# An FFT-convolution block and a four-way scan on one core: big transfers cut into parts on SyncE's queue, a new pace for background work, another order on ScalarE, and softplus operands two slices ahead

## The chip, the cores and the metric

The kernel runs on one core of a Trainium2 chip. The core has five engines with a queue of instructions each: TensorE (PE in the profile, its weight loads PEld), VectorE (DVE), ScalarE (ACT), GpSimd (POOL) and SyncE (SP), which here only issues transfers. 16 DMA engines move data between HBM and the on-chip memory SBUF. PSUM is a second, smaller on-chip memory that TensorE writes. The metric is the device time of one execution in microseconds (us).

## The reference

The input x has shape (16, 64, 64, 96): 16 images, 64 x 64 pixels, 96 channels, float32. Two layers follow, each added to its input.

```
# group norm with 32 groups: gn(x) = (x - mean) / sqrt(var + 1e-5)
# layer 0
xu  = upsample_2x(gn(x))              # by FFT, low-pass
h   = xu @ W1.T + b1                  # 96 -> 384
h   = c0 + c1 * h + c2 * h * h
h   = h @ W2.T + b2                   # 384 -> 96
x   = x + lowpass(h)[::2, ::2]        # by FFT
# layer 1
xz  = gn(x) @ in_proj.T               # 96 -> 2 * 192
u   = silu(conv3x3_depthwise(xz[:192])); z = silu(xz[192:])
# four directions k: rows, columns, and both reversed; L = 4096 steps
dt, B, C = split(x_proj[k] @ u_k)     # 6 + 16 + 16 rows
delta    = softplus(dt_proj[k] @ dt + bias)
h_t = exp(delta_t * A) * h_{t-1} + delta_t * u_t * B_t     # 192 channels x 16 states
y_t = sum over states of h_t * C_t,  + u_t * D
y   = layernorm(sum of the four directions) * z
x   = x + y @ out_proj.T
```

The softplus is computed as max(s, 0) + log(1 + e) with e = exp(-|s|), less the rounding error of 1 + e, which is ((1 + e) - 1) - e.

## The kernel before

**Three kinds of work.** `front(mi)` computes layer 0 of image mi, and of layer 1 the group norm, the projection and the 3x3 convolution; it leaves `xs`, `z` and `x1` in HBM. `scan()` runs the recurrences of all images. `finish(mi)` adds the directions, normalises, multiplies by z and projects out. `front(0)` runs alone before the scan and `finish(15)` alone after it; all the other fronts and finishes run as background inside the scan.

**The scan.** A step is an image, a pair of directions and a piece of 1024 of the 4096 positions: 16 x 2 x 4 = 128 steps. A step has 6 blocks of 64 channels (two directions of 192), a block 4 units of 4 of the 16 states, so there are 3072 units. The loop body of a unit n has two columns, e = 1 (odd) and e = 0, each a tile of 128 (32 channels x 4 states) x 1024 positions. `decay` (L719, ScalarE) makes da = exp(delta * A) in PSUM. `drive` (L725, GpSimd) makes b = dtu * B for both columns, two units ahead. `recur` (L734, L736, VectorE) runs the recurrence over a column: the odd column's result goes into b in SBUF, the even one's into da in PSUM. `keep` (L742, ScalarE) copies the last state, one element a partition, for the next step. The product with C is made by GpSimd in place for the odd column (L863), and by VectorE for the even one (L873). L863 overwrites what `keep` reads, so it waits for it. `read_out` (L758, TensorE) sums over states.

**The order of the work is written out by hand** (a manual schedule): the order of the lines is the order of each engine's queue. The background work is cut into slices, Python generators that yield between slices. `slot()` stands three times in the body of a unit: after the odd column's recurrence, after the even one's, and at the body's end. At each, `Background.slot` runs one slice where the work is behind its pace: `SLICES` slices in `POS` = 576 slots an image for `front` of the next image and then `finish` of the last; and `PSLICES` slices in 58 slots for `project`, the projections of the next step. `drain` runs what is left.

**`project`** (L633 to L671) works on pieces of 512 positions, two a step, and in each on three blocks of 128 rows: 128 x 2 x 3 = 768 blocks. A block is a matmul into `s` (PSUM), Abs and Exp on ScalarE into `e`, Ln into `d`, then on VectorE L657 (d = max(s, 0) + d), on ScalarE L659 (s = e + 1), on VectorE L661 (s = (s - 1) - e), L662 (s = d - s) and L666 (dtu = s * u), and the copy L668. `e` and `d` are in SBUF. The two results go to HBM on SP's queue, and come back spread over partitions through `fetch`.

**Queues of the transfers.** Nearly all transfers are issued by SP. Seven an image, the large ones, are issued by ScalarE: `xt` (L241, 1.5 MB, in runs of 64 elements), the two `s` (L408), `x1` (L431), `col` (L492, 2 MB) and the two `ycol` (L507, L508).

**Norms.** L227 and L252 in `norm` and `front` are small VectorE additions and products of two SBUF tiles, run three times an image.

Of the kernel before, what the change touches and what calls it, by code (L numbers as in the profile page):

```python
# [45 lines left out]
F32 = mybir.dt.float32  # L46
AF = mybir.ActivationFunctionType
ALU = mybir.AluOpType
# [3 lines left out]
C = 96  # L52
HW = 64
# [17 lines left out]
POS = 3 * 8 * 6 * NQ  # L71
SLICES = 404
PSLICES = 60


@with_exitstack
def tile_two_blocks(
    ctx: ExitStack, tc: tile.TileContext,
    x, w1, w1t, b1, w2t, b2, coef, inpt, convw, convb, xpt, dtw, alog, dsk, onw, onb, opt,
    up, down, fold, ident, gmask, pmat, bumps, out,  # L80
# [109 lines left out]
    def piece(shape, name):  # L190
        return b2p.tile(shape, F32, name=name, tag="piece")

    def norm(xt):

        s = small.tile([C, 8], F32, name="gs")
        for t in range(8):
            junk = piece([C, TB], "junk")
            nc.scalar.activation(junk, xt[:, TB * t:TB * t + TB], AF.Identity, accum_out=s[:, t:t + 1])
            if t % 2:
                yield  # L200
        yield
        m_ps = bank([C, 8], "m_ps")
        nc.tensor.matmul(m_ps, lhsT=gmask_s, rhs=s, start=True, stop=True)
        yield
        junk8 = small.tile([C, 8], F32, name="junk8")
        nmean = small.tile([C, 1], F32, name="nmean")
        nc.scalar.activation(junk8, m_ps, AF.Identity, scale=-1.0, accum_out=nmean)
        s2 = small.tile([C, 8], F32, name="gs2")
        for t in range(8):
            junk = piece([C, TB], "junk")  # L210
            nc.scalar.activation(
                junk, xt[:, TB * t:TB * t + TB], AF.Square, bias=nmean, accum_out=s2[:, t:t + 1]
            )
# [12 lines left out]
        yield  # L226
        nc.vector.tensor_mul(nb, nmean, rg)  # L227
        yield
        return rg, nb

    def front(mi):

        x_c = x[mi].rearrange("h c w -> c h w")
        x_h = x[mi]
# [5 lines left out]
        xt = b16.tile([C, L], F32, name="xt", tag="b16")  # L240
        nc.scalar.dma_start(out=xt.rearrange("c (h w) -> c h w", w=HW), in_=x_c)  # L241
        for _ in range(4):
            yield
        rg, nb = yield from norm(xt)
# [200 lines left out]
        for i, n, tiles, both in ((0, 128, 8, 0), (1, 64, 4, 4)):  # L445
            col = b16.tile([128, tiles * TB], F32, name="col", tag="b16")
            parts = [(n * k, t0) for k, t0 in enumerate((0, both)[:128 // n])]
            turned = None

            def turn(t, row, z):  # L450
                nc.scalar.copy(
                    col.rearrange("c (w h) -> c w h", w=HW)[:, :, 8 * t:8 * t + 8],
                    row.rearrange("c (h w) -> c w h", w=HW),
                )
                for p, t0 in parts:
                    cols = slice(TB * (t + t0), TB * (t + t0) + TB)
                    nc.sync.dma_start(out=made["xs"][2 * i, 0:n, cols], in_=row[p:p + n])
                    nc.sync.dma_start(out=made["z"][128 * i:128 * i + n, cols], in_=z[p:p + n])

            for t in range(tiles):  # L460
                c_ps = bank([128, 8, HW], "c_ps")
                for tap in range(9):
                    dy, dx = divmod(tap, 3)
                    for p, t0 in parts:
                        h0 = 8 * (t + t0) + dy
# [10 lines left out]
                for p, t0 in parts:  # L476
                    h0 = 8 * (t + t0) + 1
# [9 lines left out]
                turned = t, row, z  # L487
                yield
            turn(*turned)
            yield  # L490
            if i == 0:
                nc.scalar.dma_start(out=made["xs"][1], in_=col)  # L492
            else:
                for p, t0 in parts:
                    to = made["xs"][2, 64:128, :].rearrange("c (w h) -> c w h", h=HW)
                    for w0 in range(0, HW, 16):
# [3 lines left out]
                        )  # L500
                        yield

    def finish(mi):

        y_d, xs_d, z_d, x1_d = (image[mi][k] for k in ("y", "xs", "z", "x1"))
        ycol = [b18.tile([128, L], F32, name="ycol0", tag="b18"), b16.tile([64, L], F32, name="ycol1", tag="b16")]
        nc.scalar.dma_start(out=ycol[0], in_=y_d[1, 0:128, :])  # L507
        nc.scalar.dma_start(out=ycol[1], in_=y_d[1, 128:DI, :])  # L508

# [9 lines left out]
        ahead = fetch_y(0)  # L519
        for _ in range(6):  # L520
            yield
        tail = None
        for t in range(8):
# [7 lines left out]
            for ob, n in ((0, 128), (1, 64)):  # L531
# [11 lines left out]
                yield  # L543
                for i in range(2):
# [10 lines left out]
                yc.append(y_ps.rearrange("c h w -> c (h w)"))  # L555
                yield

# [3 lines left out]
            nc.tensor.matmul(v_ps, lhsT=mean_s, rhs=sq[0], start=True, stop=False)  # L561
            yield
# [5 lines left out]
            yield  # L568
            r = sq[0][0:C]
# [3 lines left out]
            for i, n in ((0, 128), (1, 64)):  # L573
                nc.tensor.matmul(o_ps, lhsT=ow_s[0:n, i, :], rhs=yz[i], start=(i == 0), stop=(i == 1))
            yield
# [4 lines left out]
            yield  # L580

# [9 lines left out]
        for _ in tail:  # L591
            yield

# [5 lines left out]
    def scan():  # L599


        with ExitStack() as es:
# [12 lines left out]
            def project(mi, pair, lc, out):  # L615
# [7 lines left out]
                for t in range(0, T, TB):  # L623
# [15 lines left out]
                    for i, v in enumerate((0, 2, 1)):  # L639
# [18 lines left out]
                        yield  # L658
                        nc.scalar.activation(s, e, AF.Identity, bias=one_s)  # L659
                        yield  # L660
                        nc.vector.scalar_tensor_tensor(s, s, -1.0, e, ALU.add, ALU.subtract)  # L661
                        nc.vector.tensor_sub(s, d, s)  # L662
                        yield
                        dtu = pj.tile([128, TB], F32, name="dtu")
# [121 lines left out]
            class Background:  # L786


                def __init__(self, gen, slices, positions):
                    self.gen, self.slices, self.positions, self.at, self.n = gen, slices, positions, 0, 0  # L790

                def slot(self):
                    self.at += 1
                    if self.gen is not None and self.n * self.positions < self.at * self.slices:
                        self.n += 1
                        if next(self.gen, 0) == 0:
                            self.gen = None

                def drain(self):
                    while self.gen is not None:  # L800
                        self.n += 1
                        if next(self.gen, 0) == 0:
                            self.gen = None

# [14 lines left out]
            for n, (st, bi, j) in enumerate(units):  # L819
# [43 lines left out]
                nc.gpsimd.tensor_mul(h, h, bc[1, r, j])  # L863
# [82 lines left out]
def _layout(i):  # L946
# [4 lines left out]
    for k in range(ND):  # L951
# [12 lines left out]
    laid = {  # L964
        "x": x,
        "w1": w1.reshape(HB, 128, C).swapaxes(0, 1),
        "w1t": w1.T,
# [35 lines left out]
```

## Time and profile before

| | us |
|---|---|
| median of 3 runs | 22337.41 (22315.87 to 22346.83) |
| the profiled execution | 22310.87 |
| its span, first to last instruction | 22309.1 |
| GpSimd busy | 20896.4 (94%) |
| VectorE busy | 19837.0 (89%) |
| TensorE busy | 15814.4 (71%) |
| ScalarE busy | 13129.1 (59%) |
| before GpSimd's first scan instruction | 532.9 |
| after its last one | 165.6 |
| DMA engines, mean rate | 191 GB/s |

The span is that of one execution, and the executions agree within some 0.15%. A line of a group gives the source line, the engine, the operation, what it writes and reads (with partitions x elements), the count, and then the busy time in us, the mean of one in ns, the idle time of the engine just ahead of these instructions, and what ended that idle time. A line of the timeline gives the start, the duration, the engine and the instruction, and in brackets the idle time before it.

### The profile page before, as it was taken

The page shows a single profiled execution, that of the slowest core. Times are in us where ns is not written, and L with a number is a line of the kernel's source. Part 1 is how long each engine was busy: PE and PEld are TensorE (multiplying, and loading weights), DVE is VectorE, ACT ScalarE, POOL GpSimd, SP SyncE. Part 2 cuts the span into 40 slices and gives each one's busy share as a digit, 9 for nine tenths or more (in the row PEclk, how much of TensorE's full clock was granted, in tenths as well). Part 3 has the DMA queues.
Part 4 walks back from the last instruction along what each step waited for, and adds up shares of the span by engine and source line. Part 5 has one row for each costly group of instructions (what it writes and reads, how often), then busy time and mean ns, then how long its engine had stood idle before and what let it go on. Part 6 is the DMA issues. An engine that isn't in the chain of part 4 may idle for free.

```text
span 22309.1 us, 261027 instructions
## 1 busy us (share of the span) xinstructions
PE 15814.4 (71%) x92844; PEld 6455.6 (29%) x92844; DVE 19837.0 (89%) x12829; ACT 13129.1 (59%) x20854; POOL 20896.4 (94%) x6152
## 2 busy tenths in 40 slices
PE   6675777767778677776777777677786777767745
PEld 4322323223232322323223232332323223232211
DVE  0999999899998999989899898999989999898996
ACT  3665655656556565565656556565565655656543
POOL 0999999999999999999999999999999999999997
PEclk7676777877778677686777878677786776867856
DMA  2555565655656556565655656556565665656654
GB/s 77 185 194 184 191 210 182 209 191 193 206 189 210 184 198 204 190 210 186 203 194 191 210 184 209 192 189 209 189 212 184 201 201 190 210 186 203 211 177 133
DMA packets 1915769, 4276.30 MB, mean 192 GB/s; under 512 B 543454, under 2 KB 642686, under 8 KB 1906206
## 3 DMA queue, kind: packets, MB, share of 16 engines
q1 hardware_dynamic: 1804702, 4086.06, 54.6%
q10 hardware_dynamic: 109760, 173.55, 3.0%
q8 instruction: 731, 11.98, 0.2%
q14 instruction: 576, 4.72, 0.1%
HBM read 3380.58 MB, written 878.18 MB: 191 GB/s over the span
## 4 chain that ended last, share of the span: by engine, by line
POOL 31%; issue 20%; DVE 20%; PE 15%; DMA 8%; ACT 5%; SPq 1%; POOLq 0%; ACTq 0%; DVEq 0%
POOL b L863 15%; POOL b L725 15%; DVE da L736 4%; DVE b L734 4%; DVE da L734 4%; DVE b L736 3%; DVE b L873 3%; PE y L758 2%; PE c_ps L466 2%; DMA u<-xs_d 2%; PE pp L633 2%; ACT da L719 2%; PE yc L535 1%; DMA ct<-rows 1%; PE oe_ps L578 1%
## 5 line engine op out<-in xcount | busy, mean ns | idle before, releaser
L725 POOL TENSOR_TENSOR b<-dtu,bt 128x2048 f32<-128x2048 f32 x3072 | 14000.3, 4557 | 578.3 <-DMA dtu<-dtu_d 531.9
L758 PE MATMUL y<-b,fold_s 128*32 128x256 f32 x49152 | 4865.1, 506 | 4962.9 <-DVE b L873 3489.3
L719 ACT ACTIVATE da<-delta,a_s 128x1024 f32<-128x1024 f32 x6144 | 6855.9, 1116 | 2487.3 <-DVE b L873 1350.0
L863 POOL TENSOR_TENSOR b<-b,ct 128x1024 f32<-128x1024 f32 x3072 | 7323.1, 2384 | 668.3 <-ACT new L742 591.3
L758 PEld LDWEIGHTS y<-b,fold_s 128*32 128x32 f32 x49152 | 1324.5, 127 | 8709.7 <-DVE b L873 4353.2
L873 DVE TENSOR_TENSOR b<-da,ct 128x1024 f32<-128x1024 f32 x3072 | 3750.4, 1221 | 75.1
L736 DVE TENSOR_TENSOR_SCAN b<-da,new,b 128x1024 f32<-128x1024 f32 x1152 | 2697.2, 2341 | 376.5 <-ACT new L742 223.5
L734 DVE TENSOR_TENSOR_SCAN b<-da,new,b 128x1024 f32<-128x1024 f32 x1152 | 2700.9, 2344 | 288.4 <-POOL b L725 283.4
L736 DVE TENSOR_TENSOR_SCAN da<-da,new,b 128x1024 f32<-128x1024 f32 x1152 | 2692.7, 2337 | 108.4 <-ACT da L719 108.4
L734 DVE TENSOR_TENSOR_SCAN da<-da,new,b 128x1024 f32<-128x1024 f32 x1152 | 2693.5, 2338 | 85.3 <-ACT da L719 85.3
L742 ACT COPY new<-da 128x1 f32<-128x1 f32 x2304 | 362.6, 157 | 3347.7 <-DVE b L873 3344.4
L466 PE MATMUL c_ps<-xgp,wtap_s 96*128 96x512 f32 (+1 forms) x4608 | 1676.9, 625 | 119.1 <-ACT row L484 114.5
L643 PE MATMUL s<-pr,dtw_s 128*128 128x512 f32 x1536 | 1202.3, 875 | 244.6 <-ACT delta L668 212.5
L358 PE MATMUL h_ps<-xu,w1t_s 96*128 96x500 f32 x1920 | 1316.4, 798 | 74.3 <-ACT hsq L341 32.8
L633 PE MATMUL pp<-u,xpt_s 128*128 128x512 f32 x1536 | 1061.8, 844 | 372.9 <-DMA u<-xs_d 359.8
L370 PE MATMUL o_ps<-w2c_s,hsq 128*100 128x96 f32 x9600 | 1222.0, 296 | 25.8 <-ACT new L742 15.1
L370 PEld LDWEIGHTS o_ps<-w2c_s,hsq 128*100 128x100 f32 x9600 | 1154.6, 208 | 284.9 <-issue 186.6
L742 ACT COPY new<-b 128x1 f32<-128x1 f32 x2304 | 429.9, 187 | 1058.2 <-DVE b L734 587.7
L657 DVE SCALAR_TENSOR_TENSOR d<-s,d 128x512 f32<-128x512 f32 x768 | 521.8, 679 | 555.6 <-ACT d L655 553.1
L736 DVE TENSOR_TENSOR_SCAN da<-da,b 128x1024 f32<-128x1024 f32 x384 | 876.5, 2282 | 133.5 <-ACT da L719 133.5
L734 DVE TENSOR_TENSOR_SCAN b<-da,b 128x1024 f32<-128x1024 f32 x384 | 876.2, 2282 | 99.3 <-POOL b L725 65.7
L736 DVE TENSOR_TENSOR_SCAN b<-da,b 128x1024 f32<-128x1024 f32 x384 | 876.5, 2283 | 69.8 <-POOL b L725 65.5
(120 smaller groups left out, 18395.2 us busy)
## 6 DMA issues: line engine op xcount, KB each, us to landing
dtu<-dtu_d SPq DMA_DIRECT2D x1536, 512.0 KB
delta<-delta_d SPq DMA_DIRECT2D x1536, 512.0 KB
bt<-rows SPq DMA_DIRECT2D x1024, 512.0 KB
ct<-rows SPq DMA_DIRECT2D x1024, 512.0 KB
u<-xs_d SPq DMA_DIRECT2D x896, 256.0 KB
dtu_d<-dtu SPq DMA_DIRECT2D x768, 256.0 KB
delta_d<-delta SPq DMA_DIRECT2D x768, 256.0 KB
xr<-in_x SPq DMA_DIRECT2D x768, 128.0 KB
```

The lines of the kernel that those rows point to most:

```text
L358: nc.tensor.matmul(h_ps[j], lhsT=w1t_s[:, 128 * j:128 * (j + 1)], rhs=xu.rearrange("c p q -> c (p q)"), start=True, stop=True,)
L370: nc.tensor.matmul(o_ps[:, p, :], lhsT=hsq[j][:, UPS * p:UPS * (p + 1)], rhs=w2c_s[:, j, :], start=(j == 0), stop=(j == HB - 1),)
L466: nc.tensor.matmul(c_ps[p:p + n], lhsT=wtap_s[:, tap, 128 * i:128 * i + n], rhs=xgp[:, h0:h0 + 8, dx:dx + HW], start=(tap == 0), stop=(tap ...
L633: nc.tensor.matmul(pp, lhsT=xpt_s[:, pair, v, :], rhs=u[v], start=(v == 0), stop=(v == 2))
L643: nc.tensor.matmul(s, lhsT=dtw_s[:, pair, v, :], rhs=pr, start=True, stop=True)
L719: nc.scalar.activation(da, ops["delta", n // NQ][:, e, :], AF.Exp, scale=a_s[:, k, g, units[n][2]:units[n][2] + 1])
L725: nc.gpsimd.tensor_mul(b, ops["dtu", n // NQ], bt.unsqueeze(1).to_broadcast([128, 2, T]))
L734: nc.vector.tensor_tensor_scan(out, da, b, before, ALU.mult, ALU.add)
L736: nc.vector.tensor_tensor_scan(out[:, ::-1], da[:, ::-1], b[:, ::-1], before, ALU.mult, ALU.add)
L758: nc.tensor.matmul(y[32 * q:32 * q + 32, e, :], lhsT=fold_s, rhs=b[:, e, QT * q:QT * q + QT], start=(pair == 0 and j == 0 and e == 0), sto ...
L863: nc.gpsimd.tensor_mul(h, h, bc[1, r, j])
L873: nc.vector.tensor_mul(bs[n][:, 0, :], h, bc[1, r, j])
```

## The change

The change has five parts.

1. A new helper `parts` cuts a large transfer into pieces along its columns, issues each on SP's queue and yields after each. `xt`, `x1`, `col` and `ycol` go through it; `s` is cut by a loop of its own, in six. The host lays out x a second time, channels first (`xc`), so that `xt` reads whole rows.
2. Slices of the convolution in `front` and of `finish` yield `HEAVY` = 2 in place of nothing, and `Background` counts what a slice yields, 1 where it yields nothing. `SLICES` goes from 404 to 540.
3. In the unit's body, `keep` of the odd column and the next unit's odd `decay` move ahead of `read_out` and of the first `slot()`.
4. In `project`, ScalarE makes 1 + e right behind Ln, in a new SBUF tile `w` in place of `s`; two empty slices follow; then VectorE makes d and w in one slice, and s = d - w and dtu in the next. A block has 7 slices instead of 8, and `PSLICES` goes from 60 to 53.
5. A local name `parts` in the convolution is renamed `halves`.

```diff
-SLICES = 404
-PSLICES = 60
+SLICES = 540
+HEAVY = 2
+PSLICES = 53
...
+    def parts(out, in_, n=4):
+
+        step = L // n
+        for i in range(n):
+            nc.sync.dma_start(out=out[:, step * i:step * i + step], in_=in_[:, step * i:step * i + step])
+            yield
...
-        nc.scalar.dma_start(out=xt.rearrange("c (h w) -> c h w", w=HW), in_=x_c)
-        for _ in range(4):
-            yield
+        yield from parts(xt, xc[mi])
+        yield
...
-        for i, on in enumerate((slice(0, JS), slice(JS, HW))):
-            nc.scalar.dma_start(out=s[i], in_=s_d[:, on, :])
-        for _ in range(8):
+        for i, n, first in [(0, JS // 4, k * JS // 4) for k in range(4)] + [(1, 10, 0), (1, 10, 10)]:
+            nc.sync.dma_start(out=s[i][:, first:first + n, :], in_=s_d[:, JS * i + first:JS * i + first + n, :])
             yield
+        yield
...
-        nc.scalar.dma_start(out=made["x1"], in_=x1)
+        yield from parts(made["x1"], x1)
...
-                        yield
+                        yield HEAVY
...
-                nc.scalar.dma_start(out=made["xs"][1], in_=col)
+                yield from parts(made["xs"][1], col)
...
-        nc.scalar.dma_start(out=ycol[0], in_=y_d[1, 0:128, :])
-        nc.scalar.dma_start(out=ycol[1], in_=y_d[1, 128:DI, :])
+        yield from parts(ycol[0], y_d[1, 0:128, :])
+        yield from parts(ycol[1], y_d[1, 128:DI, :], 2)
...
-        for _ in range(6):
-            yield
+        for _ in range(2):
+            yield HEAVY
...
-                        e = pj.tile([128, TB], F32, name="e")
-                        d = pj.tile([128, TB], F32, name="d")
+                        e, d, w = (pj.tile([128, TB], F32, name=k) for k in ("e", "d", "w"))
                         nc.scalar.activation(e, s, AF.Abs)
                         nc.scalar.activation(e, e, AF.Exp, scale=-1.0)
                         yield
                         nc.scalar.activation(d, e, AF.Ln, bias=one_s)
+                        nc.scalar.activation(w, e, AF.Identity, bias=one_s)
+                        for _ in range(2):
+                            yield
+                        nc.vector.scalar_tensor_tensor(d, s, 0.0, d, ALU.max, ALU.add)
+                        nc.vector.scalar_tensor_tensor(w, w, -1.0, e, ALU.add, ALU.subtract)
                         yield
-                        nc.vector.scalar_tensor_tensor(d, s, 0.0, d, ALU.max, ALU.add)
-                        yield
-                        nc.scalar.activation(s, e, AF.Identity, bias=one_s)
-                        yield
-                        nc.vector.scalar_tensor_tensor(s, s, -1.0, e, ALU.add, ALU.subtract)
-                        nc.vector.tensor_sub(s, d, s)
-                        yield
+                        nc.vector.tensor_sub(s, d, w)
...
                 def slot(self):
                     self.at += 1
                     if self.gen is not None and self.n * self.positions < self.at * self.slices:
-                        self.n += 1
-                        if next(self.gen, 0) == 0:
-                            self.gen = None
+                        self.step()
+
+                def step(self):
+                    weight = next(self.gen, 0)
+                    if weight == 0:
+                        self.gen = None
+                    else:
+                        self.n += weight or 1
...
                 recur(n, 1, h)
+                keep(n, 1, h)
+                if n < last:
+                    decay(n + 1, 1)
                 if n:
                     read_out(n - 1)
                 slot()
-                keep(n, 1, h)
-                if n < last:
-                    decay(n + 1, 1)
```

More of the change, by code (lines that the diff above doesn't have):

```diff
@@ L78, in tile_two_blocks @@
     ctx: ExitStack, tc: tile.TileContext,
-    x, w1, w1t, b1, w2t, b2, coef, inpt, convw, convb, xpt, dtw, alog, dsk, onw, onb, opt,
+    x, xc, w1, w1t, b1, w2t, b2, coef, inpt, convw, convb, xpt, dtw, alog, dsk, onw, onb, opt,
     up, down, fold, ident, gmask, pmat, bumps, out,
@@ L231, in front @@
     def front(mi):
-        x_c = x[mi].rearrange("h c w -> c h w")
         x_h = x[mi]
@@ L446, in front @@
             col = b16.tile([128, tiles * TB], F32, name="col", tag="b16")
-            parts = [(n * k, t0) for k, t0 in enumerate((0, both)[:128 // n])]
+            halves = [(n * k, t0) for k, t0 in enumerate((0, both)[:128 // n])]
             turned = None
@@ L454, in turn @@
                 )
-                for p, t0 in parts:
+                for p, t0 in halves:
                     cols = slice(TB * (t + t0), TB * (t + t0) + TB)
@@ L463, in front @@
                     dy, dx = divmod(tap, 3)
-                    for p, t0 in parts:
+                    for p, t0 in halves:
                         h0 = 8 * (t + t0) + dy
@@ L473, in front @@
                     if tap % 3 == 2 and tap < 8:
-                        yield
+                        yield HEAVY
                 z_ps = bank([128, 8, HW], "z_ps")
-                for p, t0 in parts:
+                for p, t0 in halves:
                     h0 = 8 * (t + t0) + 1
@@ L487, in front @@
                 turned = t, row, z
-                yield
+                yield HEAVY
             turn(*turned)
-            yield
+            yield HEAVY
             if i == 0:
-                nc.scalar.dma_start(out=made["xs"][1], in_=col)
+                yield from parts(made["xs"][1], col)
             else:
-                for p, t0 in parts:
+                for p, t0 in halves:
                     to = made["xs"][2, 64:128, :].rearrange("c (w h) -> c w h", h=HW)
@@ L500, in front @@
                         )
-                        yield
+                        yield HEAVY
     def finish(mi):
@@ L519, in finish @@
         ahead = fetch_y(0)
-        for _ in range(6):
-            yield
+        for _ in range(2):
+            yield HEAVY
         tail = None
@@ L542, in finish @@
                     nc.scalar.activation(sq[0], yc[0], AF.Square)
-                yield
+                yield HEAVY
                 for i in range(2):
@@ L555, in finish @@
                 yc.append(y_ps.rearrange("c h w -> c (h w)"))
-                yield
+                yield HEAVY
             v_ps = bank([C, TB], "v_ps")
@@ L561, in finish @@
             nc.tensor.matmul(v_ps, lhsT=mean_s, rhs=sq[0], start=True, stop=False)
-            yield
+            yield HEAVY
             yz.append(piece([64, TB], "yz"))
@@ L567, in finish @@
                 ahead = fetch_y(t + 1)
-            yield
+            yield HEAVY
             r = sq[0][0:C]
@@ L574, in finish @@
                 nc.tensor.matmul(o_ps, lhsT=ow_s[0:n, i, :], rhs=yz[i], start=(i == 0), stop=(i == 1))
-            yield
+            yield HEAVY
             e_ps = bank([C, TB], "oe_ps")
@@ L579, in finish @@
             nc.vector.tensor_mul(r, o_ps, r)
-            yield
+            yield HEAVY
             def end(r, e_ps, cols):
@@ L591, in finish @@
         for _ in tail:
-            yield
+            yield HEAVY
     blocks = [(0, 0, 0), (0, 2, 0), (2, 0, 0), (2, 2, 1), (1, 0, 1), (1, 2, 1)]
@@ L655, in project @@
                         nc.scalar.activation(d, e, AF.Ln, bias=one_s)
-                        yield
-                        nc.vector.scalar_tensor_tensor(d, s, 0.0, d, ALU.max, ALU.add)
-                        yield
-                        nc.scalar.activation(s, e, AF.Identity, bias=one_s)
-                        yield
-                        nc.vector.scalar_tensor_tensor(s, s, -1.0, e, ALU.add, ALU.subtract)
-                        nc.vector.tensor_sub(s, d, s)
-                        yield
+                        nc.scalar.activation(w, e, AF.Identity, bias=one_s)
[3 more added lines that the diff above has]
+                        nc.vector.scalar_tensor_tensor(w, w, -1.0, e, ALU.add, ALU.subtract)
+                        yield
+                        nc.vector.tensor_sub(s, d, w)
                         dtu = pj.tile([128, TB], F32, name="dtu")
@@ L794, in slot @@
                     if self.gen is not None and self.n * self.positions < self.at * self.slices:
-                        self.n += 1
-                        if next(self.gen, 0) == 0:
-                            self.gen = None
+                        self.step()
[5 more added lines that the diff above has]
+                        self.n += weight or 1
                 def drain(self):
                     while self.gen is not None:
-                        self.n += 1
-                        if next(self.gen, 0) == 0:
-                            self.gen = None
+                        self.step()
             nothing = Background(None, 0, 1)
@@ L965, in _layout @@
         "x": x,
+        "xc": x.transpose(0, 2, 1, 3).reshape(-1, C, L),
         "w1": w1.reshape(HB, 128, C).swapaxes(0, 1),
```

## The prediction

> **What bounds the kernel now.** I read the page first, then the groups of GpSimd (POOL) with their releasers, then the busy time by stage, then two stretches of the timeline. Of the page, the busy shares:
>
> ```profile
> PE 15814.4 (71%) x92844; PEld 6455.6 (29%) x92844; DVE 19837.0 (89%) x12829; ACT 13129.1 (59%) x20854; POOL 20896.4 (94%) x6152
> ```
>
> POOL leads, DVE (VectorE) is close behind. The groups of POOL say what its idle time waits for:
>
> ```profile
> L725 POOL TENSOR_TENSOR b<-dtu,bt 128x2048 f32<-128x2048 f32 x3072 | 14000.3, 4557 | 578.3 <-DMA dtu<-dtu_d 531.9 <-PE y L758 21.2 <-issue 9.6
> L863 POOL TENSOR_TENSOR b<-b,ct 128x1024 f32<-128x1024 f32 x3072 | 7323.1, 2384 | 668.3 <-ACT new L742 591.3 <-DVE b L736 65.7 <-DMA u<-xs_d 4.8
> ```
>
> The 531.9 us is one wait, the first image's front part before the scan. The rest is about 715 us, of which 591.3 us is L863 waiting for the tiny state copy (L742) on ScalarE. The busy time by stage (before the scan, scan, after it; last a plain stretch of the second image, where POOL never waits):
>
> ```profile
> 0.00:532.90 532.90, 370.18 (x2238) 227.09 (x2238) 23.69 (x61) 204.81 (x325) 0.48 (x8) 0.79 0.25 70
> 532.90:22143.50 21610.60, 15297.59 (x90302) 6185.94 (x90302) 19795.75 (x12744) 12899.10 (x20488) 20895.87 (x6144) 0.74 0.59 195
> 22143.50:22309.10 165.60, 146.64 (x304) 42.60 (x304) 17.58 (x25) 25.22 (x41) 0.01 (x1) 0.90 0.34 97
> 2030.00:2640.00 610.00, 435.24 (x3002) 207.40 (x3003) 569.20 (x360) 361.52 (x574) 610.00 (x180) 0.71 0.55 185
> ```
>
> (Columns: PE, PEld, DVE, ACT, POOL busy, clock, DMA share, GB/s.) In the scan POOL works 20895.9 of 21610.6 us: 3072 units of 6.80 us, one L725 and one L863 each. DVE works 19795.8 us, so it has only 1815 us to give; in the plain stretch 41 us of 610.
>
> The next rows decide my forecast. L252 adds two SBUF tensors of 96x96 on DVE. With POOL idle, then beside POOL:
>
> ```profile
> 45.26 0.24 DVE L252 TENSOR_TENSOR lin<-lin,ident_s 96x96 f32<-96x96 f32 x1
> ...
> 604.52 2.34 POOL L863 TENSOR_TENSOR b<-b,ct 128x1024 f32<-128x1024 f32 x1 [0.54 <-ACT new L742]
> 604.72 0.14 DVE L251 TENSOR_TENSOR shift<-k_ps,cb_s 96x1 f32<-96x1 f32 x1
> 604.78 2.19 DVE L252 TENSOR_TENSOR lin<-lin,ident_s 96x96 f32<-96x96 f32 x1
> 606.83 4.52 POOL L725 TENSOR_TENSOR b<-dtu,bt 128x2048 f32<-128x2048 f32 x1
> ```
>
> 0.24 us alone, 2.19 us beside POOL, and it ends 0.1 us after POOL's instruction. L251 just ahead, with one input in PSUM, takes 0.14 us. L227, again two SBUF inputs (96x1):
>
> ```profile
> 8114.60 4.54 POOL L725 TENSOR_TENSOR b<-dtu,bt 128x2048 f32<-128x2048 f32 x1
> 8116.89 9.00 DVE L227 TENSOR_TENSOR nb<-nmean,rg 96x1 f32<-96x1 f32 x1
> 8119.07 2.37 POOL L863 TENSOR_TENSOR b<-b,ct 128x1024 f32<-128x1024 f32 x1
> 8121.37 4.52 POOL L725 TENSOR_TENSOR b<-dtu,bt 128x2048 f32<-128x2048 f32 x1
> 8132.48 2.36 POOL L863 TENSOR_TENSOR b<-b,ct 128x1024 f32<-128x1024 f32 x1 [6.59 <-ACT new L742]
> ```
>
> It stood through three POOL instructions; then POOL itself ran dry for 6.59 us, since the scan behind L227 on DVE was late. Of 45 such instructions beside POOL (30 of L227, 15 of L252), 40 ended with the POOL instruction they met and 5 took 9.00 us. Their mean is 2.76 us against 0.185 us alone, so 2.58 us of waiting each.
>
> **The change, part by part.**
>
> *Softplus.* Before, each of 768 blocks ran four DVE instructions (L657, L661, L662, L666), each with `s` in PSUM as one input. After, 1 + e goes into a new SBUF tile `w`. The first instruction (`d`) and the last (`dtu`) still read PSUM. But `w <- w, e` and `s <- d, w` have both inputs in SBUF. That is 768 x 2 = 1536 new instructions of the kind of L252 and L227, at 0.68 us of work each (rows L661, L662: 680 and 696 ns). No row shows one of this size, so I bound its wait. Below, nothing: DVE may take its turn while POOL is idle. Above, 9.0 us less the work. I take 2.58 us, the mean of the 45, which met the same POOL instructions: 1536 x 2.58 = 3960 us more on DVE. How long POOL is kept off by such an instruction no row shows either, L252 being too short; the bounds are 0 and its 0.68 us, 1044 us in all. I put it at nothing in the sum, since where DVE is the bound POOL has idle time to give.
>
> DVE then needs 19796 + 3960 = 23756 us in a scan of 21611 us, 2145 us too much. In the plain stretch: 610 us are 3.6 steps of 24 units with 12 such instructions each, 43 x 2.58 = 111 us against 41 us to spare. Two corrections. DVE does not use all its time: about a quarter of each step has no softplus slices, DVE there needs two scans of 2.34 and a product of 1.22, 5.9 us of a 6.80 us unit, and it can run ahead of POOL's L863 by no more than L725 of the unit ahead lets it, 6.80 - 2.36 = about 4.4 us; I put 1.5 us lost in each of 128 steps, +190 us. And POOL, idle for (23756 - 20896) / 23756 = 12% of the scan, holds DVE up less often: -12% of 3960, -475 us. Sum: 2145 + 190 - 475 = +1860 us.
>
> The Trainium skill, page SBUF — State Buffer, section Who interferes with whom, speaks against this edit: a DVE instruction with two SBUF inputs and a GpSimd one that reads SBUF exclude each other, and the second to issue is blocked until the first finishes. By that rule the wait ends with the instruction met, on average (4.557² + 2.384²) / (2 x 6.80) = 1.94 us, an estimate that would make the first product 2987 us and the sum about +1000 us; the 9.00 us rows show that a waiting instruction can also be passed over.
>
> The two empty slices between Ln and the DVE part remove the wait "DVE d L657 <- ACT d L655", 553.1 us in all, 128 of them ahead of the scan. That is DVE time, and the sum above already counts DVE as never idle. ScalarE's `delta` copy now stands behind a DVE instruction that may be late; what queues behind it is the state copy, and DVE's scans are late by then anyway.
>
> *State copy and decay of the odd column ahead of the slot.* `keep` and `decay` go ahead of the read-out and of one background slice in three. Nothing is added: 0.19 and 1.12 us of ACT in another order, and the background slice is later by 1.3 us. This takes from the 591.3 us; at most all of it, at least nothing, since slices of the two earlier slots still stand ahead. I take 400 us with the next part. POOL's gaps are then no longer ACT's, but they are DVE's: where DVE is the bound this gives nothing beyond the sum.
>
> *Transfers.* Seven ACT issues an image (16 images, 112 at 0.3 to 0.5 us) become 24 on SP: `xt` 4, `s` 6, `x1` 4, `col` 4, `ycol` 6. At 0.35 us that is 384 x 0.35 = 134 us of SP. Queued behind them on SP are the fetches of dtu, delta, bt, ct, y0 and u; those of dtu and delta are issued a block of four units (27 us) early, which hides a part of 0.5 MB (2.6 us at 195 GB/s). If that cover were gone, each late part would cost POOL some 3 us, 384 x 3 = 1150 us at most. The ycol parts wait on SP for the release of the col buffer. What they remove: in 14 images POOL stood 11 to 14 us once (14 x 12.0 = 168 us) when 3 MB of `ycol` delayed the u tiles; part of the 400 us. Of the front and the tail outside the scan (532.9 and 165.6 us), the x load changes its queue and layout: 10 us either way, taken as 0.
>
> *Pace.* Before: front 265 light and 58 heavy slices, finish 72, 395 in all at 404/576 = 0.70 a slot. After: front 273 + 2 x 58 = 389, finish 6 + 2 x 68 = 142, 531 of 540 at 0.94 a slot. The front ends at slot 415 instead of 461, the whole at 566 as before. Light slices come 1.34 times as dense; PE in the plain stretch goes from 71% to some 80% and stays hidden.
>
> Sum: 22309 + 1860 = 24169 us; the profiled execution took 22310.9 us, 27 us under the median of the runs, which is about the 0.2% that a measurement tells. I say 24,200 us.
>
> **The rivals.**
> A (0.62): as above, DVE with its waits is the bound. 23,500 to 25,700 us; the top adds POOL's 1044 us in series and some passed-over cases.
> B (0.18): DVE's lead hides the ordinary waits, as it did for 40 of the 45, and only passed-over ones cost, 6.6 us each: 1536 x 5/45 x 6.6 = 1126 us, less 400 us. 23,000 us (22,700 to 23,500). Against it: 12 in each step leave no time to rebuild the lead.
> C (0.11): such an instruction is passed over one time in three: 1536 x (1/3 - 1/9) x 6.8 = 2320 us more, 26,500 us. For it: the arbitration is seen only 45 times, with tiny tiles.
> D (0.09), the other side: the waits of the 96-row tiles do not carry over to these, the edits do what they say. 22311 less up to 591.3 us, about 21,750 us. It decides if a contended instruction costs the path under 400 / 1536 = 0.26 us. Of its share 0.07 is faster, 0.02 a tie.
>
> **How the numbers follow.** The range leaves out C and D (0.20) and holds A and B: 22,750 to 25,700 us. A alone: 23,500 to 25,700. Faster 0.07, within 0.2% 0.02, slower 0.91.
>
> **What would show it.** Right: the new `w` and `s` instructions on DVE average 2.5 to 3.5 us instead of 0.68, ending with POOL's; DVE busy at 96% or more; POOL's L863 waits for the scans, its unit near 7.6 us; L742's 591.3 us mostly gone; the gaps of 11 to 14 us gone. Wrong: those groups near 0.7 us and POOL at 97% (D), or POOL's own instructions longer by 0.68 us with DVE not late (POOL pays, between B and A).

## The result and the profile after

The changed kernel takes 24,661.66 us (median of 4 runs, 24,641.04 to 24,680.47) against 22,342.12 us before; the ratio is 1.1039, with an interval of 1.102 to 1.1059. It is slower by 2,320 us, the way that was forecast, and 460 us beyond the point forecast of 24,200 us. The page of the profile after, its span and busy shares:

```profile
span 24654.1 us, 261341 instructions
PE 15766.8 (64%) x92844; PEld 6518.6 (26%) x92844; DVE 23032.6 (93%) x12829; ACT 13103.8 (53%) x20854; POOL 21233.2 (86%) x6152
```

VectorE (DVE) now leads with 23,033 us, 3,196 us more than before, although it runs the same 12,829 instructions. GpSimd (POOL) fell from 94% to 86%. The groups of POOL, with the idle time ahead of them and who ended it:

```profile
L729 POOL TENSOR_TENSOR b<-dtu,bt 128x2048 f32<-128x2048 f32 x3072 | 14044.8, 4572 | 602.8 <-DMA dtu<-dtu_d 511.0
L871 POOL TENSOR_TENSOR b<-b,ct 128x1024 f32<-128x1024 f32 x3072 | 7419.5, 2415 | 2654.2 <-ACT new L746 1945.7
```

(L729 and L871 are the L725 and L863 of before.) POOL's own instructions are nearly as long as they were; its idle time ahead of the product with C went from 668 to 2,654 us. The releaser named is still ScalarE's state copy, but the copy of the odd column's state itself waits for the recurrence of VectorE (L738 and L740, before L734 and L736): the idle time ahead of it went from 1,058 to 2,869 us, 1,432 of it behind L740 and 1,428 behind L738.

```profile
L742 ACT COPY new<-b 128x1 f32<-128x1 f32 x2304 | 429.9, 187 | 1058.2 <-DVE b L734 587.7 <-DVE b L736 440.7 <-DMA delta_d<-delta 20.1
```

```profile
L746 ACT COPY new<-b 128x1 f32<-128x1 f32 x2304 | 432.8, 188 | 2869.4 <-DVE b L740 1431.7
```

The groups of VectorE say why the recurrence is late. The two instructions on 1 + e before, with s in PSUM, and then the four of a block after:

```profile
L661 DVE SCALAR_TENSOR_TENSOR s<-s,e 128x512 f32<-128x512 f32 x768 | 521.9, 680 | 65.7 <-ACT s L659 65.7
L662 DVE TENSOR_TENSOR s<-d,s 128x512 f32<-128x512 f32 x768 | 534.4, 696 | 26.3
```


```profile
L665 DVE SCALAR_TENSOR_TENSOR w<-w,e 128x512 f32<-128x512 f32 x768 | 2697.4, 3512 | 0.0
L667 DVE TENSOR_TENSOR s<-d,w 128x512 f32<-128x512 f32 x768 | 1578.5, 2055 | 0.2
L670 DVE TENSOR_TENSOR dtu<-s,u 128x512 f32<-128x512 f32 x768 | 530.8, 691 | 26.3
L664 DVE SCALAR_TENSOR_TENSOR d<-s,d 128x512 f32<-128x512 f32 x768 | 518.2, 675 | 187.7 <-ACT d L660 187.7
```

Four instructions of one shape stand side by side in the second table. The two that have an input in PSUM take 0.675 and 0.691 us. The two with both inputs in SBUF take 3.512 and 2.055 us. Their surplus is 768 x (3.512 - 0.68 + 2.055 - 0.68) = 3,230 us, about what VectorE gained in busy time (3,196 us). The work is the same as before, so this surplus is waiting: the profile records it inside the instruction's duration, and VectorE counts as busy while it waits. One of the longer cases in the timeline:

```profile
720.83 4.51 POOL L729 TENSOR_TENSOR b<-dtu,bt 128x2048 f32<-128x2048 f32 x1
721.10 0.67 DVE L664 SCALAR_TENSOR_TENSOR d<-s,d 128x512 f32<-128x512 f32 x1
721.69 10.95 DVE L665 SCALAR_TENSOR_TENSOR w<-w,e 128x512 f32<-128x512 f32 x1
725.30 2.33 POOL L871 TENSOR_TENSOR b<-b,ct 128x1024 f32<-128x1024 f32 x1
727.60 4.48 POOL L729 TENSOR_TENSOR b<-dtu,bt 128x2048 f32<-128x2048 f32 x1
732.56 2.35 DVE L738 TENSOR_TENSOR_SCAN da<-da,new,b 128x1024 f32<-128x1024 f32 x1
734.82 0.67 DVE L667 TENSOR_TENSOR s<-d,w 128x512 f32<-128x512 f32 x1
```

L664 runs beside POOL's product and is not disturbed. L665, the next one, is held through three instructions of POOL, until POOL has nothing ready; it ends 0.55 us after the third. Then L667, with two SBUF inputs as well, meets an idle POOL and takes 0.67 us. The busy time by stage, the scan and the plain stretch that was shown of before (PE, PEld, DVE, ACT, POOL busy, clock, DMA share, GB/s):

```profile
511.99:24490.67 23978.68, 15258.35 (x90302) 6251.37 (x90302) 22991.82 (x12744) 12873.88 (x20488) 21232.72 (x6144) 0.72 0.53 176
2030.00:2640.00 610.00, 387.87 (x3024) 206.96 (x3024) 587.19 (x313) 333.46 (x570) 526.37 (x154) 0.72 0.47 157
```

In that stretch POOL worked 610 of 610 us before and ran 180 instructions; now it works 526 us and runs 154. VectorE is at 587 of 610.

### The profile page after: what moved, and what is told of

It reads as the page before. It is cut to its first block, busy times and chain, and to the rows that moved or that the text cites. A ratio compares the mean times of both kernels' runs of the same rounds, so it can differ in the third digit from the quotient of the medians.

```text
span 24654.1 us, 261341 instructions
## 1 busy us (share of the span) xinstructions
PE 15766.8 (64%) x92844; PEld 6518.6 (26%) x92844; DVE 23032.6 (93%) x12829; ACT 13103.8 (53%) x20854; POOL 21233.2 (86%) x6152
## 4 chain that ended last, share of the span: by engine, by line
DVE 38%; issue 22%; POOL 19%; PE 8%; ACT 6%; DMA 6%; SPq 1%; POOLq 0%; DVEq 0%; ACTq 0%
POOL b L729 12%; DVE w L665 9%; POOL b L871 7%; DVE da L740 6%; DVE da L738 6%; DVE s L667 5%; DVE b L740 4%; DVE b L738 4%; ACT da L723 2%; DVE b L881 2%; PE pp L639 2%; DMA ct<-rows 2%; DVE d L664 1%; DMA u<-xs_d 1%; PE y L762 1%
## 5 line engine op out<-in xcount | busy, mean ns | idle before, releaser
L729 POOL TENSOR_TENSOR b<-dtu,bt 128x2048 f32<-128x2048 f32 x3072 | 14044.8, 4572 | 602.8 <-DMA dtu<-dtu_d 511.0
L871 POOL TENSOR_TENSOR b<-b,ct 128x1024 f32<-128x1024 f32 x3072 | 7419.5, 2415 | 2654.2 <-ACT new L746 1945.7
L762 PE MATMUL y<-b,fold_s 128*32 128x256 f32 x49152 | 4626.7, 501 | 5110.2 <-DVE b L881 4469.4
L762 PEld LDWEIGHTS y<-b,fold_s 128*32 128x32 f32 x49152 | 1471.5, 131 | 8539.3 <-DVE b L881 5288.1
L738 DVE TENSOR_TENSOR_SCAN da<-da,new,b 128x1024 f32<-128x1024 f32 x1152 | 2694.1, 2339 | 142.6 <-ACT da L723 142.4
L738 DVE TENSOR_TENSOR_SCAN b<-da,new,b 128x1024 f32<-128x1024 f32 x1152 | 2696.7, 2341 | 122.0 <-POOL b L729 109.9
L740 DVE TENSOR_TENSOR_SCAN da<-da,new,b 128x1024 f32<-128x1024 f32 x1152 | 2693.8, 2338 | 116.7 <-ACT da L723 116.7
L740 DVE TENSOR_TENSOR_SCAN b<-da,new,b 128x1024 f32<-128x1024 f32 x1152 | 2697.2, 2341 | 107.9 <-POOL b L729 106.5
L665 DVE SCALAR_TENSOR_TENSOR w<-w,e 128x512 f32<-128x512 f32 x768 | 2697.4, 3512 | 0.0
L472 PE MATMUL c_ps<-xgp,wtap_s 96*128 96x512 f32 (+1 forms) x4608 | 1922.1, 709 | 97.9 <-ACT row L490 93.3
L667 DVE TENSOR_TENSOR s<-d,w 128x512 f32<-128x512 f32 x768 | 1578.5, 2055 | 0.2
L364 PE MATMUL h_ps<-xu,w1t_s 96*128 96x500 f32 x1920 | 1210.7, 733 | 275.9 <-ACT hsq L347 161.1
L376 PEld LDWEIGHTS o_ps<-w2c_s,hsq 128*100 128x100 f32 x9600 | 1080.6, 197 | 331.9 <-ACT hsq L347 139.8
L639 PE MATMUL pp<-u,xpt_s 128*128 128x512 f32 x1536 | 975.8, 784 | 124.0 <-DMA u<-xs_d 111.9
L740 DVE TENSOR_TENSOR_SCAN da<-da,b 128x1024 f32<-128x1024 f32 x384 | 876.1, 2282 | 150.1 <-ACT da L723 150.1
L472 PEld LDWEIGHTS c_ps<-xgp,wtap_s 96*128 96x128 f32 (+1 forms) x4608 | 668.0, 192 | 1235.1 <-issue 1044.1
```

What stands on the lines that cost most here:

```text
L376: nc.tensor.matmul(o_ps[:, p, :], lhsT=hsq[j][:, UPS * p:UPS * (p + 1)], rhs=w2c_s[:, j, :], start=(j == 0), stop=(j == HB - 1),)
L472: nc.tensor.matmul(c_ps[p:p + n], lhsT=wtap_s[:, tap, 128 * i:128 * i + n], rhs=xgp[:, h0:h0 + 8, dx:dx + HW], start=(tap == 0), stop=(tap ...
L639: nc.tensor.matmul(pp, lhsT=xpt_s[:, pair, v, :], rhs=u[v], start=(v == 0), stop=(v == 2))
L665: nc.vector.scalar_tensor_tensor(w, w, -1.0, e, ALU.add, ALU.subtract)
L667: nc.vector.tensor_sub(s, d, w)
L729: nc.gpsimd.tensor_mul(b, ops["dtu", n // NQ], bt.unsqueeze(1).to_broadcast([128, 2, T]))
```

## The experiments

The theory: VectorE's instructions with two SBUF inputs can not run beside POOL's products, which read SBUF, so they wait, VectorE becomes late, and POOL then waits for it. The rivals: the transfers or the pace make the loss; or the new place of the softplus in the order does.

### The softplus alone, and everything but the softplus

The first is the kernel before with part 4 of the change alone (the diff of `project` shown with the change, and `PSLICES = 53`). The second is the changed kernel with the old softplus:

```diff
-PSLICES = 53
+PSLICES = 60
...
-                        nc.scalar.activation(w, e, AF.Identity, bias=one_s)
-                        for _ in range(2):
-                            yield
+                        yield
                         nc.vector.scalar_tensor_tensor(d, s, 0.0, d, ALU.max, ALU.add)
-                        nc.vector.scalar_tensor_tensor(w, w, -1.0, e, ALU.add, ALU.subtract)
-                        yield
-                        nc.vector.tensor_sub(s, d, w)
+                        yield
+                        nc.scalar.activation(s, e, AF.Identity, bias=one_s)
+                        yield
+                        nc.vector.scalar_tensor_tensor(s, s, -1.0, e, ALU.add, ALU.subtract)
+                        nc.vector.tensor_sub(s, d, s)
+                        yield
```

> The kernel before with the softplus part of the change alone (w in SBUF, two empty slices, PSLICES 53); transfers, pace and the order of keep and decay as before. Theory (VectorE's instructions with two SBUF inputs wait for GpSimd's): the whole loss is here, and the gains of the other parts are missing, so no faster than the changed kernel's 24,662 us: 24,700 us (24,400 to 25,200), the instructions on w and s at about 3.5 and 2.1 us each. Rival (the transfers on SyncE's queue or the new pace make the loss): near 22,340 us, within 300 us, with w and s at 0.7 us.

> The changed kernel with the old softplus (PSLICES 60 again), all other parts kept. Theory: the loss is gone and the gains show: 21,900 us (21,700 to 22,100), GpSimd's wait for the state copy under 250 us instead of 591 us. Rival (transfers or pace make the loss): 24,000 us or more.

The softplus alone took 24,887.84 us, a ratio of 1.1135 (1.1118 to 1.1151), with w at 2.96 and s at 2.56 us. With the softplus undone the kernel took 22,114.41 us, 0.9894 (0.988 to 0.9909), so a gain of 233 us. The whole loss is in the softplus; transfers, pace and the new place of `keep` are cleared. That gain lies just short of the range expected (22,114 us where 22,100 was the upper end, and POOL's wait for the state copy at 278 us instead of under 250). It is the same size beside the loss: 24,888 - 24,662 = 226 us. The prices of w and s lie nearer to each other than the 3.5 and 2.1 us expected; their sum is 5.5 us, as in the changed kernel (5.6).

### The same instructions, one operand moved to PSUM

```diff
-                        nc.vector.scalar_tensor_tensor(w, w, -1.0, e, ALU.add, ALU.subtract)
+                        nc.vector.scalar_tensor_tensor(w, s, -1.0, e, ALU.add, ALU.subtract)
                         yield
-                        nc.vector.tensor_sub(s, d, w)
+                        nc.vector.tensor_sub(s, s, w)
```

> The changed kernel with the same instructions in the same order on every engine, but the two VectorE instructions read s in PSUM as their first input in place of w and d in SBUF; the result of max and Ln and the rounding term are thereby left out of the softplus. Theory (the two SBUF inputs are the cause, nothing else in the new order): both instructions at 0.68 us, 21,800 us (21,600 to 22,000), GpSimd at 95% busy or more. Rival (the new order of the softplus, its two empty slices or VectorE's later start, makes the loss): 24,662 us within 300 us.

It took 21,846.58 us, 0.9779 (0.9764 to 0.9793): 2,815 us less than the changed kernel, with the same instructions on every engine and only one operand of two of them in the other memory. Its groups of VectorE, and POOL's:

```profile
L665 DVE SCALAR_TENSOR_TENSOR w<-s,e 128x512 f32<-128x512 f32 x768 | 523.6, 682 | 0.0
L667 DVE TENSOR_TENSOR s<-s,w 128x512 f32<-128x512 f32 x768 | 522.2, 680 | 0.2
```

```profile
L729 POOL TENSOR_TENSOR b<-dtu,bt 128x2048 f32<-128x2048 f32 x3072 | 13979.5, 4551 | 547.8 <-DMA dtu<-dtu_d 512.8 <-PE y L762 12.3 <-DVE b L740 12.2
L871 POOL TENSOR_TENSOR b<-b,ct 128x1024 f32<-128x1024 f32 x3072 | 7300.7, 2377 | 235.2 <-ACT new L746 173.4 <-DVE b L738 55.9 <-DVE b L740 2.4
```

Both are at 0.67 to 0.70 us in every case, whatever POOL does, and POOL's wait for the state copy is 173 us. This settles the cause: it is the second SBUF operand beside a busy POOL, not the place in the order. The order itself is a gain: 22,114 - 21,847 = 268 us against the old softplus in the same kernel (some 220 us with the whole softplus, in `mended2` below).

### One contended instruction in each block

`only_w` adds max and Ln in place in PSUM, so that just the instruction on w has two SBUF inputs. `only_s` lets the instruction on w read s in PSUM, as above, and keeps the last one.

```diff
 only_w
-                        nc.vector.scalar_tensor_tensor(d, s, 0.0, d, ALU.max, ALU.add)
+                        nc.vector.scalar_tensor_tensor(s, s, 0.0, d, ALU.max, ALU.add)
...
-                        nc.vector.tensor_sub(s, d, w)
+                        nc.vector.tensor_sub(s, s, w)
 only_s
-                        nc.vector.scalar_tensor_tensor(w, w, -1.0, e, ALU.add, ALU.subtract)
+                        nc.vector.scalar_tensor_tensor(w, s, -1.0, e, ALU.add, ALU.subtract)
```

> The changed kernel where only the instruction on w has two SBUF inputs: max and Ln are added in place in PSUM, and the last one subtracts w from s there. Theory (each such instruction waits for the GpSimd instruction that it meets, and a late VectorE leaves GpSimd dry, so that the second of a block often meets nothing): the first of a block keeps its price, w at 3.3 to 3.6 us, s at 0.68, and most of the loss stays: 23,500 us (23,200 to 24,000) against 21,847 with none and 24,662 with both. Rival (each of the two costs half): 23,250 us or less with w under 3 us.

> The changed kernel where only the last one, s from d and w, has two SBUF inputs; the instruction on w reads s in PSUM, so the rounding term is wrong and left out. Theory (the second is cheap in the changed kernel, 2.06 us, because the first has already made GpSimd run dry): alone it meets a running GpSimd, its mean goes up to 2.7 to 3.6 us, and the time is 23,400 us (23,000 to 23,900). Rival (its price is its own, by its place behind the recurrence): the mean stays at 2.06 us and the time is 21,847 + 2815 x 1.37 / (2.83 + 1.37) = 22,770 us.

Measured: 23,902.58 us (1.0704, 1.0689 to 1.0719) and 23,872.64 us (1.069, 1.0675 to 1.0704). The contended group of VectorE, of `only_w` and then of `only_s`:

```profile
L665 DVE SCALAR_TENSOR_TENSOR w<-w,e 128x512 f32<-128x512 f32 x768 | 2943.0, 3832 | 0.0
```

```profile
L667 DVE TENSOR_TENSOR s<-d,w 128x512 f32<-128x512 f32 x768 | 2923.1, 3806 | 0.2
```

Each alone waits 3.1 us and costs some 2,040 us; both together cost 2,815, not 4,080. The s instruction went from 2.06 to 3.81 us when it stood alone, beyond the upper end of what was expected; w, at 3.83 us, also lies above the 3.3 to 3.6 us expected for it. So its low price in the changed kernel is not its own: of its 762 cases in the scan 329 met an idle POOL, because w had made VectorE late; alone, 3 did.

### Both directly behind one another

```diff
-                        nc.vector.scalar_tensor_tensor(w, w, -1.0, e, ALU.add, ALU.subtract)
                         yield
+                        nc.vector.scalar_tensor_tensor(w, w, -1.0, e, ALU.add, ALU.subtract)
                         nc.vector.tensor_sub(s, d, w)
```

> The changed kernel with the two contended instructions directly behind one another in one slice (the first moves one slice later). Theory (the shared way to SBUF goes back to GpSimd at the first one's end): the second waits for a whole GpSimd instruction, s at 3 us or more, and the time is 24,700 us or more. Rival (VectorE keeps it from one to the next, or GpSimd has run dry by then): s at 0.68 us, and the time falls to that of the one contended instruction, 23,900 us (23,600 to 24,200).

25,144.54 us (1.1259, 1.1242 to 1.1276), w at 4.12 and s at 1.83 us. The time went as the theory said, the mean of s did not. Case by case it is split: 374 times POOL was idle and s took 0.70 us; in the other 388 POOL had an instruction ready, started it as w ran, and s waited for its end (2.72 us in each of 351 cases). So in none of these 388 cases did VectorE keep the way to SBUF from one instruction to the next.

### The other parts one by one

`keep_alone` is the kernel before with part 3 alone. `parts_and_pace` is the kernel before with parts 1 and 2 alone (`parts`, `HEAVY` and `SLICES = 540` as in the change, the old softplus, the old place of `keep`).

```diff
 keep_alone
                 recur(n, 1, h)
+                keep(n, 1, h)
+                if n < last:
+                    decay(n + 1, 1)
                 if n:
                     read_out(n - 1)
                 slot()
-                keep(n, 1, h)
-                if n < last:
-                    decay(n + 1, 1)
```

> The kernel before with keep and decay of the odd column ahead of the read-out and the first slot, nothing else. Theory (background slices ahead of the state copy on ScalarE make most of GpSimd's 591 us): 22,150 us (21,950 to 22,300), that wait at 250 to 400 us. Rival (the slices of the two earlier slots and the large transfers make it): 22,340 us, no difference over 0.2%.

> The kernel before with the transfers in parts on SyncE's queue and the new pace, nothing else. Theory (the large transfers on ScalarE's queue delay the u tiles once an image): the gaps of 11 to 14 us are gone, 168 us of them, 22,180 us (22,050 to 22,300). Rival (what SyncE waits for now, or the light slices 1.34 times as dense, takes this back): 22,340 us or more, with new gaps of GpSimd in units 0 to 110 of an image, where there were few.

`keep_alone`: 22,423.23 us, 1.0039 (1.0026 to 1.0051), slower by 95 us, where 22,150 us, a gain, was expected. `parts_and_pace`: 21,943.95 us, 0.9829 (0.9816 to 0.9843), a gain of 385 us, more than twice what was expected (22,180 us). The two longest rows of the waits of POOL behind other engines in the second (sum in us, times, longest):

```profile
POOL b L873 <- ACT new L748: 202.9, 147, 4.0
POOL b L873 <- DVE b L740: 55.9, 15, 3.7
```

The longest gap behind the state copy is 4.0 us where it was 14.0, and their sum went from 591 to 203 us. The 14 gaps of over 11 us, 168 us, are gone; most of the rest comes from units 112 to 159, where the convolution's slices ran 1.5 times as dense before. Some gaps appear earlier in the image (about 190 us in units 80 to 111, which had none), where layer 1's norm and the first part of the convolution now lie. Of these, 56 us are the second row above: 15 waits for the recurrence behind L235 (L227 of the kernel before), the small product with two SBUF inputs, which took 6.0 us at that place in each of 15 images. Moving `keep` and `decay` ahead of the slot gave nothing on the kernel before: POOL's wait for the copy fell to 430 us, but only since the 14 long gaps, all over 8 us, now stand ahead of the other product (L725) with another releaser; without them it was 591 - 168 = 423 us before. VectorE's wait for Ln rose, from 553 to 682 us, as its group shows:

```profile
L657 DVE SCALAR_TENSOR_TENSOR d<-s,d 128x512 f32<-128x512 f32 x768 | 525.0, 684 | 700.1 <-ACT d L655 682.2 <-ACT new L742 16.4
```

which fits that every slice's ScalarE work now stands behind a decay of 1.1 us; that this makes the loss is argued, not shown.

### Versions without the contention

`mended` lets ScalarE make w - 1 in one more instruction. `mended2` needs none: each of three instructions takes one input from SBUF and one from PSUM.

```diff
 mended
+    mone_s = const.tile([128, 1], F32, name="mone_s")
+    nc.gpsimd.memset(mone_s, -1.0)
...
+                        nc.scalar.activation(w, w, AF.Identity, bias=mone_s)
...
-                        nc.vector.scalar_tensor_tensor(d, s, 0.0, d, ALU.max, ALU.add)
-                        nc.vector.scalar_tensor_tensor(w, w, -1.0, e, ALU.add, ALU.subtract)
+                        nc.vector.scalar_tensor_tensor(s, s, 0.0, d, ALU.max, ALU.add)
+                        nc.vector.tensor_sub(s, s, w)
                         yield
-                        nc.vector.tensor_sub(s, d, w)
+                        nc.vector.tensor_add(s, s, e)
```

```diff
 mended2
-                        nc.vector.scalar_tensor_tensor(d, s, 0.0, d, ALU.max, ALU.add)
-                        nc.vector.scalar_tensor_tensor(w, w, -1.0, e, ALU.add, ALU.subtract)
+                        nc.vector.scalar_tensor_tensor(s, s, 0.0, d, ALU.max, ALU.add)
+                        nc.vector.scalar_tensor_tensor(s, w, -1.0, s, ALU.add, ALU.subtract)
                         yield
-                        nc.vector.tensor_sub(s, d, w)
+                        nc.vector.tensor_sub(s, e, s)
```

`mended2_oldkeep` is `mended2` with part 3 undone, and `mended2_oldkeep_nb` moves also the small product of L235 to ScalarE:

```diff
-        nc.vector.tensor_mul(nb, nmean, rg)
+        nc.scalar.activation(nb, nmean, AF.Identity, scale=rg)
```

> The changed kernel with the softplus rearranged so that every VectorE instruction has s in PSUM as one input: ScalarE makes w - 1 in one more instruction, VectorE makes s = max(s, 0) + d, s - w and s + e, and dtu. Four VectorE instructions a block as before, one more of ScalarE (768 x 0.68 = 520 us, at 53 to 59% busy). Theory: 21,800 us (21,600 to 22,050), faster than both kernels. Rival (more work on ScalarE or the empty slices cost the path): 22,340 us or more.

> The changed kernel with the whole softplus and no additional instruction: s = max(s, 0) + d in PSUM, s = (w - 1) - s, s = e - s, each with one input in SBUF and one in PSUM. Theory: as with the operand in PSUM, 21,850 us (21,780 to 21,920), 150 us under the version with one more ScalarE instruction. Rival (the order of the inputs matters, a second input in PSUM being read otherwise): the two instructions above 0.75 us and more than 22,000 us.

> The same with keep and decay of the odd column back behind the slot. Theory (that move costs, as it did by itself, 95 us on the kernel before and 170 us beside transfers and pace): 21,700 us (21,620 to 21,780). Rival (with the softplus ahead, the move no longer costs, since Ln has two slices more to come): 21,850 us or more.

> The same with the small product of L235 made by ScalarE, so that the scan has but 15 VectorE instructions with two SBUF inputs left. Theory: these 30 cost GpSimd 15 gaps of 3.7 us in the run with the operand in PSUM, so 55 us less, 21,640 us (21,560 to 21,720). Rival (hidden): no difference over 0.2% to the one above.

| version | us, median | ratio to before, interval |
|---|---|---|
| mended | 21,998.12 | 0.9844 (0.9827 to 0.986) |
| mended2 | 21,892.33 | 0.9805 (0.9788 to 0.9821) |
| mended2_oldkeep | 21,914.74 | 0.9813 (0.9799 to 0.9828) |
| mended2_oldkeep_nb | 21,861.59 | 0.979 (0.9775 to 0.9804) |

All four beat both kernels. One more ScalarE instruction a block costs some 90 us by the ratios, 106 us by the medians. The move of `keep` makes no difference to speak of once the softplus runs ahead (22 us or 0.1%, and the intervals overlap; the rival's case, the 21,700 us expected were wrong): its cost beside the old softplus does not carry over. Taking L235 from VectorE brings 53 us (0.24%), the difference that was expected; the time of 21,640 us was missed with the one above it. In the waits of `mended2_oldkeep` stands the row

```profile
POOL b L871 <- DVE b L738: 52.2, 14, 3.7
```

which is no longer there in the last version: so much did these 30 tiny instructions cost POOL, in 14 gaps.

## Why the prediction was right

The measured time lies in the range and in case A, DVE with its waits as the bound. Point by point:

| term of the sum | predicted, us | measured, us |
|---|---|---|
| waits of the 1536 instructions on DVE | 3960 - 475 = 3485 | 3230 |
| VectorE idle in the scan | 190 | 23,979 - 22,992 = 987 |
| scan | 21,611 + 1860 = 23,471 | 23,979 |
| outside the scan | 698 | 675 |
| span | 24,169 | 24,654 |

- **The price of a contended instruction.** 2.58 us less the correction was right within 8% as a mean, though it came from tiles of 96 rows and 1 or 96 columns. That is in part luck. The single prices differ: w waits 2.83 us, s 1.37, and the forecast that both lie at 2.5 to 3.5 us failed for s. Nor do such waits add up; a late VectorE makes POOL idle, and beside an idle POOL s took 0.67 us. The -12% was too small a correction for the second of a pair and too large for the first: it takes the meetings as random, and while POOL was idle for 11% of the scan, w met an idle POOL 28 times of 762 and s 329 times. Alone in a block, each waits 3.1 us, a fifth above 2.58.
- **VectorE is never idle but for 190 us.** This is the step that was mis-sized, by about 800 us, the largest error of the sum; the waits, put 255 us too high, take a part of it back. In the scan VectorE still waits some 530 us for decays of ScalarE and some 325 us for POOL's b:

```profile
DVE da L740 <- ACT da L723: 266.8, 181, 3.2
DVE da L738 <- ACT da L723: 182.9, 151, 2.4
DVE b L740 <- POOL b L729: 166.3, 202, 2.1
DVE b L738 <- POOL b L729: 158.3, 181, 1.1
```

  These waits stood in the profile before, at some 490 us each (four rows of them below); the sum counted VectorE as never idle but for 190 us of another kind and priced none of them:

```profile
DVE b L734 <- POOL b L725: 349.1, 474, 1.1
DVE da L736 <- ACT da L719: 242.0, 152, 4.5
DVE da L734 <- ACT da L719: 146.5, 80, 5.1
DVE b L736 <- POOL b L725: 144.3, 187, 1.1
```

  A bound taken as busy without a gap is a floor. The wait for Ln, which the change was to remove, is down from 392 to 28 us in the scan. (Ahead of the scan it was 161 us in all before; the 128 us of the prediction are the longest one, and no term rests on it.)
- **POOL is held for between 0 and 0.68 us, taken as 0.** Where VectorE got its turn and POOL's next instruction was ready, that one took 2.78 instead of 2.36 us or 4.98 instead of 4.53; 645 of them, about 280 us over the run. Small, and partly beside other waits.
- **Passed-over instructions.** 102 of 1536 stood through more than one POOL instruction, all of them on w, for up to 11.2 us; what they waited beyond the first one is some 640 of the 3,230 us. By the Trainium skill, page SBUF — State Buffer, section Who interferes with whom, the second to issue is blocked until the first finishes. The pair of engines and the two SBUF inputs are just what the runs show. That it takes a GpSimd instruction that reads SBUF is not shown here, since both of POOL's products read and write it; and the 102 cases are not in the rule. The prediction's estimate by that rule, 2987 us of waits, comes as near to the 3230 measured as its own 3485 does. The sum of about +1000 us that went with it was too low against the +2,345 of the spans, since it too left out most of VectorE's idle time, and the rows' +1860 is nearer.
- **Transfers, pace and the order of `keep`, 400 us together.** `parts_and_pace` gives 385 us, `keep_alone` takes 95 us, together 233. That the move of `keep` adds nothing anywhere was wrong. And "gives nothing beyond the sum where DVE is the bound" was wrong too: the 226 us are gained beside the loss.
- **Rivals.** B (23,000 us) fails since VectorE's lead is used up: in the plain stretch POOL went from 610 to 526 us. C fails as 102 of 1536 were passed over, not a third. D fails at the result itself: w and s average 3.5 and 2.1 us, not 0.7.
- **What was to be seen.** VectorE at 96% of the scan: 22,992 / 23,979 = 95.9%. The unit at 7.6 us: 7.81. That the state copy's share of POOL's waits would mostly go was wrong by name: it rose to 1,946 us, since the copy passes on the lateness of the recurrence. The gaps of 11 to 14 us are gone, as forecast: the longest one behind the copy is 8.4 us.

## What to carry to other kernels

Before an operand of a VectorE instruction is moved from PSUM to SBUF, look whether GpSimd is busy at that time: two SBUF inputs then turned 0.68 us into 2 to 4 us on average, and with one input in PSUM it stayed at 0.68 us. Rare small instructions of the same kind in the trace show the price ahead of the change; compare their duration beside GpSimd with that beside an idle one. Look in the profile before for the waits of the engine that is to become the bound; those that the change does not remove belong in the sum. Run the parts of a change one by one: here a gain of 385 us, one of 268 us and a loss of 95 us were hidden under one operand.

## What was not expected of the hardware

- A VectorE instruction that waits for GpSimd may be passed over where GpSimd has its next one ready: in the changed kernel 102 of the 466 such waits of w. In the other 231 GpSimd had nothing ready that could pass it. What decides among the 466 stays open. The phase alone does not (cases of both kinds start 0.7 to 3 us into the instruction that they meet), but one place can behave the same in every image: in `parts_and_pace` L235 was passed over at the later of its two places in 15 images of 15, and at the earlier one in none.
- Two contended instructions in sequence do not hold GpSimd off: it slipped in between in all 388 cases in which it had work.
- Moving 1.3 us of ScalarE work ahead of a slot made the kernel before slower by 0.4%, and made no difference after the softplus ran two slices ahead.
